# Inverse square roots of the norms by a power on GpSimd and one Newton step

## Chip, cores and metric

The kernel runs on one core of one Trainium2 chip. The metric is the device time of one execution in microseconds (us), a median of repeated runs. Engines are named as in the profile: PE is TensorE (PEld its weight loads), DVE is VectorE, ACT is ScalarE, POOL is GpSimd, SP is the engine that issues most transfers.

## The reference, cut to what matters

The input x has 8 batches of 1024 rows of 256 values, in float32. An attention block is followed by a feed-forward block, each with a residual and a layer norm after it.

```python
q, k, v = x @ Wq.T + bq, x @ Wk.T + bk, x @ Wv.T + bv      # 16 heads of 16
q = softmax(q, axis=-1)                                    # over the 16 values of a head
k = softmax(k, axis=-2)                                    # over the 1024 rows
out = q @ (k.T @ v)                                        # per head
out = (out - mean(out)) * rsqrt(var(out) + EPS) * ln_g + ln_b
x = layernorm(x + out @ Wo.T + bo)

h = layernorm(x) * ln1_g + ln1_b
h = gelu(h @ ternary(w1).T + b1)                           # 256 -> 1024, exact gelu
h = layernorm(h) * ln2_g + ln2_b
x = layernorm(x + h @ ternary(w2).T + b2)                  # 1024 -> 256
```

`ternary(w)` rounds w over its mean absolute value to -1, 0 or 1 and scales it back. Every layer norm needs 1/sqrt(var + EPS) of each row.

## The kernel before

**Tiling.** A batch lies in SBUF with 128 rows on the partitions and NT = 8 row tiles of 256 columns. Four tiles are a block of 512 rows, so there are 16 blocks, two per batch. All matmuls are in float32 or its fp32r form.

**Order.** The order of all instructions is written out by hand (`manual_schedule`). One loop runs over 18 iterations i. In the first 16, block i gets its keys, queries and the product of keys and x; in even iterations the state of the batch before is finished; and block i - 2 gets its attention output (`attend`). Iterations 16 and 17 have only `attend` left, and the feed-forward's slots are mixed in.

**The norm's steps.** `attend` puts a short generator (`bn_stats`, then `bn_aggr`) in the queue `soon`. When both blocks of a batch are through, a generator `norm(b, tiles)` is put in the queue `later`. It issues one VectorE instruction per step: var + EPS for all tiles (L519), `rsqrt` for these n = 8 columns (tiles `ny_o`, `nt_o`), then for each tile the scaled residual add (L526), statistics (L532) and their aggregate (L534), then two rows of variances (L539, L541), `rsqrt` for these 2n = 16 columns (`ny_y`, `nt_y`; the second half serves the feed-forward's entry norm), then sh (L546) and two products for rs2 (L549, L551). After it, ScalarE applies the norm to the tiles (L772), a few at a time through `apply(n)`. Norms of batches 0 to 6 have 8 tiles, that of batch 7 comes in two halves of 4. `more(n)` advances the queues by n steps, `soon` first; the step that ends a generator also advances the next queue. An even iteration of the attention hands out 1, 4, 4, 4, 1, 4, 6, 6, 6, 1 and 6 steps.

**Around it.** In an attention iteration VectorE takes the maxima of the keys (mx, L326), from which mb and nb (L333, L335) give the bias of ScalarE's exponentials (ekT, L338), whose transposes (pte, L351) TensorE waits for. It adds the bias of the queries (q, L368) out of PSUM, takes their maxima (qm, L377) and sums (rq, L388 and L390). GpSimd subtracts the maxima (L378), multiplies by the inverse sums (L391) and issues a transfer that adds a constant row to x (L855). A preparation of the quantised weights is spread over the first ten iterations (`prep`; among it mean of L179 and the columns of L194).

**Feed-forward.** Blocks go through slots s, eight per block, numbered by m = s + 11 for the hidden layer. A slot holds matmuls into the hidden layer (ph, L615 and L619), ScalarE's gelu (L620), a turn of a hidden tile (pt, L643) split into a high and a low part (ScalarE L568, VectorE L569), and the product with the second weights (pf, L657). At m % 8 = 0 `enter` gives GpSimd two passes over the next block (L576, L579). At m % 8 = 5 and 6 the input of the next block is turned (pth, L592) and split in the same way (hT, L568 and L569). At s % 8 = 2 `norms` issues `rsqrt` without a break for one vector of 8 columns: four of the result's norm of the block before, four of the hidden norm (`ny_f`, `nt_f`). At s % 8 = 3 `finish` applies the former on GpSimd (four times L670) and stores the block; sc and ms (L706, L708) come from the latter. After the last slot one more `rsqrt` of 4 columns (`ny_last`) leads to the last `finish`.

There are 35 inverse square roots in all: 9 of `ny_o`, 9 of `ny_y`, 16 of `ny_f` and `ny_last`.

Of the kernel before, what the change touches and what calls it, by code (L numbers as in the profile page):

```python
# [7 lines left out]

F32 = mybir.dt.float32
I32 = mybir.dt.int32  # L10
F32R = mybir.dt.float32r
AF = mybir.ActivationFunctionType
ALU = mybir.AluOpType
AX = mybir.AxisListType

P = 128
EPS = 1e-5
ROUND = 12582912.0
RSQRT_SEED = float(0x5F3759DF)


@with_exitstack
def attn_ffn_postln_kernel(
# [11 lines left out]
    nc = tc.nc  # L35
# [6 lines left out]
    NT = N // P  # L42
# [4 lines left out]
    const = ctx.enter_context(tc.tile_pool(name="const", bufs=1))  # L47
# [59 lines left out]
    def finish_all(steps):  # L107

        while True:
            try:  # L110
                next(steps)
            except StopIteration as end:
                return end.value

    def rsqrt(v, name):


        n = v.shape[1]
        y = small.tile([P, 2 * NT], F32, tag="ny", name=f"ny_{name}")[:, :n]
        t = small.tile([P, 2 * NT], F32, tag="nt", name=f"nt_{name}")[:, :n]  # L120
        yi = y.bitcast(I32)
        nc.vector.tensor_scalar(yi, v.bitcast(I32), 1, None, ALU.logical_shift_right)
        yield
        nc.vector.tensor_scalar(yi, yi, -1.0, RSQRT_SEED, ALU.mult, ALU.add)
        for step in range(3):
            yield
            nc.vector.tensor_tensor(t, y, y, ALU.mult)  # L127
            yield
            nc.vector.scalar_tensor_tensor(t, t, -0.5, v, ALU.mult, ALU.mult)
            yield  # L130
            nc.vector.scalar_tensor_tensor(y, t, 1.5, y, ALU.add, ALU.mult)
        return y


# [379 lines left out]
    def norm(b, tiles):  # L514
# [4 lines left out]
        nc.vector.tensor_scalar(v, mvo[b][:, lo:hi, 1], EPS, None, ALU.add)  # L519
        yield  # L520
        rs = yield from rsqrt(v, f"o_{b}_{lo}")
        yield
        mv = small.tile([P, NT, 2], F32, tag="mvy", name=f"mvy_{b}_{lo}")[:, :n, :]
# [17 lines left out]
        nc.vector.tensor_scalar(v[:, n:], mv[:, :, 1], 1.0 + EPS, EPS * EPS, ALU.mult, ALU.add)  # L541
        yield
        rs = yield from rsqrt(v, f"y_{b}_{lo}")
        yield
        sh = small.tile([P, NT], F32, tag="shy", name=f"shy_{b}_{lo}")[:, :n]
# [143 lines left out]
    def norms(s):  # L689

        i, j = s // HC, s % HC
        if j in (0, 1) and i > 0:
            result_stats(i - 1, 2 * j)
            result_stats(i - 1, 2 * j + 1)
        if i == len(blocks):
            return
        if j == 2:
            v = small.tile([P, 2 * G], F32, tag="nv", name=f"nv_f_{i}")
            nc.vector.tensor_scalar(v[:, :G], mv[i][:, :G, 1], EPS, None, ALU.add)
            nc.vector.tensor_scalar(v[:, G:], mv[i][:, G:, 1], 1.0 / HID, EPS, ALU.mult, ALU.add)  # L700
            rs[i] = finish_all(rsqrt(v, f"f_{i}"))
        if j == 3:
            if i > 0:
                finish(i - 1, mv[i][:, :G, 0], rs[i][:, :G])
            sc[i] = small.tile([P, G], F32, tag="sc", name=f"sc_{i}")
            nc.vector.tensor_scalar(sc[i], rs[i][:, G:], inv2, None, ALU.mult)  # L706
            ms[i] = small.tile([P, G], F32, tag="ms", name=f"ms_{i}")
            nc.vector.tensor_tensor(ms[i], sc[i], mv[i][:, G:, 0], ALU.mult)  # L708
        if j in (4, 5):
            add_mean(i, 2 * j - 8)  # L710
            add_mean(i, 2 * j - 7)
# [204 lines left out]
```

## Time and profile before

| what | value |
|---|---|
| time, median of 3 runs | 741.25 us (739.79 to 741.45) |
| profiled execution: its own time | 739.53 us |
| profiled execution: span of the instructions | 737.8 us |
| mean granted TensorE clock | 0.978 |
| TensorE matmul / weight load busy | 690.7 / 549.1 us |
| VectorE busy | 583.7 us, 1642 instructions |
| ScalarE busy | 441.0 us |
| GpSimd busy | 194.8 us, 156 instructions |
| HBM traffic | 31 GB/s over the span |

How to read the profile: a line of a group names the source line, the engine, the operation, output and inputs, the count, the busy time and the mean of one in ns, then the idle time of that engine just before and what released it. A line of the order of time gives the start in us, the time in us, and the instruction, with the idle time before it and its releaser in brackets. A line of the chain of waits gives the start, the time, and which instruction held the end back then. The attention runs to about 348 us, the last `attend` and the first feed-forward slots to about 420, the feed-forward alone to about 712.

### The profile page before, as it was taken

The numbers are of one execution on the slowest core, as the hardware profiler recorded it, in microseconds if no ns is written. First come the engines' busy times: TensorE is split into PE (matmuls) and PEld (weight loads), VectorE is DVE, ScalarE is ACT, GpSimd is POOL, SyncE is SP. The second block draws the span as 40 slices with busy tenths as digits, with TensorE's granted clock in tenths as the row PEclk, the third lists the DMA queues.
The fourth block names the chain that finished last, engine by engine and source line by source line (L and its number), as shares of the span: only waits on it lengthen the run. The fifth ranks groups of instructions, "written<-read, shape, count | busy, mean of one in ns | idle before, by whom it ended". The sixth has DMA issues, their size and how long they took to land.

```text
span 737.8 us, 10770 instructions
## 1 busy us (share of the span) xinstructions
PE 690.7 (94%) x3780; PEld 549.1 (74%) x3780; DVE 583.7 (79%) x1642; ACT 441.0 (60%) x970; POOL 194.8 (26%) x156
## 2 busy tenths in 40 slices
PE   6899999979989999997998899999999999999992
PEld 4677766757657777765767788888888888888882
DVE  1667798877988959797898778877878877887686
ACT  2344436535364545546787667777777677677760
POOL 1232223121221222244420033332133333123112
PEclk9999999989999999998999899999999999999997
DMA  8833103222120111210100000000000000000001
GB/s 328 306 72 58 29 15 72 51 36 51 21 33 13 29 29 28 30 24 11 24 0 2 1 29 30 30 29 30 1 29 30 28 29 30 2 28 29 30 30 58
DMA packets 17238, 32.03 MB, mean 43 GB/s; under 512 B 1344, under 2 KB 12608, under 8 KB 16288
## 3 DMA queue, kind: packets, MB, share of 16 engines
q0 software_dynamic: 8608, 8.79, 7.9%
q1 hardware_dynamic: 7344, 21.50, 7.7%
q10 hardware_dynamic: 1232, 1.06, 0.4%
q8 instruction: 30, 0.49, 0.3%
q14 instruction: 24, 0.20, 0.1%
HBM read 14.56 MB, written 8.39 MB: 31 GB/s over the span
## 4 chain that ended last, share of the span: by engine, by line
PE 70%; DVE 23%; ACT 3%; DMA 2%; issue 2%; POOL 0%; POOLq 0%; ACTq 0%; DVEq 0%
PE pf L657 16%; PE ph L615 14%; PE pt L643 7%; PE po L498 6%; PE pq L364 5%; PE pa L407 5%; PE pk L322 5%; PE ph L619 3%; DVE x L526 3%; DVE st_y L532 2%; DMA wqkv_sb<-in_wqkv_dram 2%; PE pth L592 2%; PE ptq L301 1%; PE ptx L301 1%; DVE sto L508 1%
## 5 line engine op out<-in xcount | busy, mean ns | idle before, releaser
L657 PE MATMUL pf<-t,u 128*128 128x256 f32 x1024 | 157.5, 295 | 4.0 <-DVE x L716 3.6
L615 PE MATMUL ph<-t,hT 128*128 128x512 f32 x512 | 144.2, 403 | 1.2 <-DVE hT L569 1.2
L657 PEld LDWEIGHTS pf<-t,u 128*128 128x128 f32 x1024 | 131.9, 191 | 9.8 <-issue 5.8
L569 DVE SCALAR_TENSOR_TENSOR u<-pt,cols_sb,u 128x512 fp32r<-128x512 f32 x128 | 95.5, 746 | 45.6 <-ACT u L568 44.2
L620 ACT ACTIVATE h<-ph 128x512 f32<-128x512 f32 x128 | 76.5, 598 | 83.9 <-PE ph L619 73.7
L670 POOL TENSOR_SCALAR x<-x,ny_f,sh 128x256 f32<-128x256 f32 x60 | 38.1, 650 | 261.0 <-DVE sh L667 261.0
L615 PEld LDWEIGHTS ph<-t,hT 128*128 128x128 f32 x512 | 88.6, 189 | 15.3 <-DVE hT L569 1.9
L498 PE MATMUL po<-sm,qT 128*128 128x384 f32 x256 | 97.3, 505 | 0.1
L568 ACT ACTIVATE u<-pt,cols_sb 128x512 fp32r<-128x512 f32 x128 | 87.5, 684 | 8.3 <-PE pt L643 7.6
L643 PE MATMUL pt<-ident,h 128*128 128x128 f32 x512 | 78.1, 275 | 4.2 <-DVE u L569 2.5
L632 ACT ACTIVATE sq<-h,mvh 128x1024 f32<-128x1024 f32 x64 | 73.8, 1153 | 5.5 <-DVE mvh L624 5.5
L643 PEld LDWEIGHTS pt<-ident,h 128*128 128x128 f32 x512 | 61.6, 141 | 19.9 <-DVE hT L569 6.0
L378 POOL TENSOR_TENSOR q<-q,qm 128x1024 f32<-128x1024 f32 x16 | 30.8, 1926 | 150.1 <-DVE qm L377 90.6
L364 PE MATMUL pq<-wqkv_sb,xT 128*128 128x256 f32 x256 | 60.6, 380 | 0.8 <-DMA wqkv_sb<-in_wqkv_dram 0.8
L322 PE MATMUL pk<-xT,wqkv_sb 128*128 128x512 f32 x128 | 61.3, 603 | 0.0
L407 PE MATMUL pa<-x,ek 128*128 128x256 f32 x256 | 61.1, 382 | 0.0
L498 PEld LDWEIGHTS po<-sm,qT 128*128 128x128 f32 x256 | 46.5, 198 | 19.4 <-issue 2.1
L391 POOL TENSOR_TENSOR q<-q,rq 128x1024 f32<-128x1024 f32 x16 | 30.9, 1933 | 108.2 <-DVE rq L390 59.0
L407 PEld LDWEIGHTS pa<-x,ek 128*128 128x128 f32 x256 | 48.9, 192 | 13.1 <-issue 0.6
L364 PEld LDWEIGHTS pq<-wqkv_sb,xT 128*128 128x128 f32 x256 | 47.9, 190 | 12.7 <-issue 3.1
L680 DVE SCALAR_TENSOR_TENSOR x<-g2sum,ms,x 128x256 f32<-128x256 f32 x64 | 56.9, 927 | 0.0
L338 ACT ACTIVATE ekT<-pk,nb 128x512 f32<-128x512 f32 x32 | 21.7, 682 | 56.5 <-DVE nt_y L127 35.6
(144 smaller groups left out, 1151.9 us busy)
## 6 DMA issues: line engine op xcount, KB each, us to landing
x<-crow POOLq DMA_DIRECT2D x16, 512.0 KB, 5.5
out_dram<-x SPq DMA_DIRECT2D x16, 512.0 KB, 2.6
x<-in_x_dram SPq DMA_DIRECT2D x7, 1024.0 KB, 10.2
x<-in_x_dram SPq DMA_DIRECT2D x2, 512.0 KB, 5.6
wm_w<-in_w_dram SPq DMA_DIRECT2D x4, 256.0 KB, 8.0
wq_w<-in_w_dram SPq DMA_DIRECT2D x4, 256.0 KB, 2.5
wm_w<-in_w_dram SPq DMA_DIRECT2D x8, 128.0 KB, 2.1
wq_w<-in_w_dram SPq DMA_DIRECT2D x8, 128.0 KB, 2.0
```

The costliest lines, as they stand in the source:

```text
L322: nc.tensor.matmul(pk, wqkv_sb[:, k, C + c * P : C + (c + 1) * P], xT[i][:, k, :], start=(k == 0), stop=(k == KC - 1),)
L364: nc.tensor.matmul(pq[:, n, :], xT[i][:, k, (t + n) * P : (t + n + 1) * P], wqkv_sb[:, k, 0:C], start=(k == 0), stop=(k == KC - 1),)
L407: nc.tensor.matmul(pa[i][:, c, :], ek[i][:, t, c * P : (c + 1) * P], x_of(i)[:, t, :], start=(t == 0), stop=(t == G - 1),)
L498: nc.tensor.matmul(po[:, c * P : c * P + P + C], qT[i][:, c, t * P : (t + 1) * P], sm[b][:, c, :], start=(c == 0), stop=(c == KC - 1), ski ...
L568: nc.scalar.activation(hi, src, AF.Copy, scale=gain)
L569: nc.vector.scalar_tensor_tensor(lo, src, gain, hi.bitcast(F32), ALU.mult, ALU.subtract)
L615: nc.tensor.matmul(ph, hT[i][s][:, k, t * P : (t + 1) * P], t1[:, k, cols_j], start=(s == 0 and k == 0), stop=False,)
L620: nc.scalar.activation(h[i][t][:, cols_j], ph, AF.Gelu, accum_out=h[i, t][:, half : half + 1])
L632: nc.scalar.activation(sq, h[i][t], AF.Square, bias=mv[i][:, G + t, 0:1], accum_out=mv[i][:, G + t, 1:2])
L643: nc.tensor.transpose(pt[:, t * P : (t + 1) * P], h[i][t][:, j * P : (j + 1) * P], ident)
L657: nc.tensor.matmul(pf[i][t // 2][:, t % 2, :], u[s][:, n, t * P : (t + 1) * P], t2[:, j, :], start=(j == 0 and t % 2 == 0 and n == 0), sto ...
L680: nc.vector.scalar_tensor_tensor(x_t, g2sum, ms[i][:, t : t + 1], x_t, ALU.mult, ALU.add)
```

## The change

`rsqrt(v)` gave a vector 1/sqrt(v) by an integer shift and a subtraction on the bits and three Newton steps of three instructions, eleven VectorE instructions with ten breaks between them. It now gives v to the power -1/2 in one GpSimd instruction, with a constant tile of -0.5 as the exponent, and one Newton step of three VectorE instructions, with three breaks. All 35 inverse square roots go through it.

```diff
-RSQRT_SEED = float(0x5F3759DF)
...
+    mhalf = const.tile([P, 2 * NT], F32, name="mhalf")
+    nc.vector.memset(mhalf, -0.5)
+
     def rsqrt(v, name):
         n = v.shape[1]
         y = small.tile([P, 2 * NT], F32, tag="ny", name=f"ny_{name}")[:, :n]
         t = small.tile([P, 2 * NT], F32, tag="nt", name=f"nt_{name}")[:, :n]
-        yi = y.bitcast(I32)
-        nc.vector.tensor_scalar(yi, v.bitcast(I32), 1, None, ALU.logical_shift_right)
-        yield
-        nc.vector.tensor_scalar(yi, yi, -1.0, RSQRT_SEED, ALU.mult, ALU.add)
-        for step in range(3):
-            yield
-            nc.vector.tensor_tensor(t, y, y, ALU.mult)
-            yield
-            nc.vector.scalar_tensor_tensor(t, t, -0.5, v, ALU.mult, ALU.mult)
-            yield
-            nc.vector.scalar_tensor_tensor(y, t, 1.5, y, ALU.add, ALU.mult)
+        nc.gpsimd.tensor_tensor(y, v, mhalf[:, :n], ALU.pow)
+        yield
+        nc.vector.tensor_tensor(t, y, y, ALU.mult)
+        yield
+        nc.vector.scalar_tensor_tensor(t, t, -0.5, v, ALU.mult, ALU.mult)
+        yield
+        nc.vector.scalar_tensor_tensor(y, t, 1.5, y, ALU.add, ALU.mult)
         return y
```

More of the change, by code (lines that the diff above doesn't have):

```diff
@@ L9 @@
 F32 = mybir.dt.float32
-I32 = mybir.dt.int32
 F32R = mybir.dt.float32r
```

## The prediction

> **What bounds the kernel now.** I read the page's busy shares first, then its chain of waits, then what waited for whom, and last the order of time on VectorE and TensorE around each inverse square root.
>
> ```profile
> PE 690.7 (94%) x3780; PEld 549.1 (74%) x3780; DVE 583.7 (79%) x1642; ACT 441.0 (60%) x970; POOL 194.8 (26%) x156
> ...
> PE 70%; DVE 23%; ACT 3%; DMA 2%; issue 2%; POOL 0%; POOLq 0%; ACTq 0%; DVEq 0%
> ```
>
> TensorE ends most of the span, but VectorE holds 23% of the chain. GpSimd is on it only at the very end. So the value of shorter VectorE work depends on the stage. The small instructions themselves, by shape:
>
> ```profile
> L127 DVE TENSOR_TENSOR nt_f<-ny_f 128x8 f32<-128x8 f32 x48 | 8.0, 167 | 1.6
> L131 DVE SCALAR_TENSOR_TENSOR ny_y<-nt_y,ny_y 128x16 f32<-128x16 f32 x21 | 3.7, 175 | 0.5
> L378 POOL TENSOR_TENSOR q<-q,qm 128x1024 f32<-128x1024 f32 x16 | 30.8, 1926 | 150.1 <-DVE qm L377 90.6 <-DVE z L425 59.5
> L905 POOL MEMSET const-float32-1.0<- 128x1 f32 x1 | 0.1, 98 | 0.0
> ```
>
> No power is in this trace. These rows give an instruction of the old chain (0.17 us), an ordinary two-input GpSimd pass (1.93 us for 1024 columns) and GpSimd's smallest instruction (0.10 us). In the feed-forward stage (420 to 712 us) one group of eight slots takes 21.9 us; this is the place of its chain, VectorE first, then the weight loads:
>
> ```profile
> 595.54 0.17 DVE L122 TENSOR_SCALAR ny_f<-nv_f 128x8 int32<-128x8 int32 x1
> 595.75 0.17 DVE L124 TENSOR_SCALAR ny_f<-ny_f 128x8 int32<-128x8 int32 x1
> ...
> 597.56 0.17 DVE L131 SCALAR_TENSOR_TENSOR ny_f<-nt_f,ny_f 128x8 f32<-128x8 f32 x1
> 597.65 0.74 DVE L569 SCALAR_TENSOR_TENSOR hT<-pth,gs,hT 128x512 fp32r<-128x512 f32 x1
> ...
> 598.45 0.42 PEld L643 LDWEIGHTS pt<-ident,h 128*128 128x128 f32 x4 [0.28 <-DVE hT L569]
> ```
>
> Eleven dependent instructions start 0.20 us apart. The hT pass queued behind them frees the PSUM buffer for which TensorE's next transposes wait. The transposes then take 0.51 us of the chain instead of 0.44: TensorE loses 0.07 us per group and has no slack. A longer chain costs its whole excess here; a shorter one gains at most 0.07.
>
> **What the skill says.** "GPSIMD Engine Reference", section "Elementwise — side-by-side cycle accounting": about 2.6 cycles per element for two inputs; the trace's 1926 ns / 1024 = 1.88 ns is 2.3 cycles at the page's 1.2 GHz, so it agrees roughly. It has no price for a power. "SBUF — State Buffer", "Who interferes with whom": a GpSimd instruction and a VectorE instruction with two SBUF inputs exclude each other. The trace agrees: the pass L526 takes 1.83 us beside the GpSimd pass at 96.08 us and 0.45 us elsewhere. "TensorE: Matmul & The Clock Gate", "HAM oscillation": idle gaps above some 3.4 us halve TensorE's clock. Here gaps of 3.70 us (before 162.2) and 3.50 us (before 334.4) are followed by half-speed stretches of 6.8 us (mean clock 0.85 and 0.87 in these windows); but so are pairs of shorter gaps (2.26 and 0.34 at 204, 3.4 us; 1.31 and 2.52 before 410, 6.8 us), so the trace is less lenient.
>
> **The round trip.** VectorE's qm ends at 95.92 and GpSimd starts at 96.08: 0.16 us. GpSimd's pass ends at 211.58 and ScalarE starts at 211.62: 0.04. So an inverse square root removes 8 x 0.20 = 1.60 us of VectorE time and adds a stall L = 0.20 + d, d being the power. Three Newton instructions stay. The constant's one memset at the start counts as nothing: VectorE is busy for 0.31 of the first 10 us, which are loads (uncovered, 0.2 us at most, the like of `ones`).
>
> Bounds of d: floor, a memset's 0.10 plus the row's 1.9 ns per column, 0.12 us. For the middle, the same skill page, "Performance pitfalls for Q7 kernels", prices a dependent fp32 step at 4 cycles. My assumption is some 20 such steps per column (a logarithm, a product, an exponential), 16 partitions of a core side by side: estimate 20 x 4 / 1.2 GHz = 67 ns per column, so d = 0.10 + 0.067n: 0.37, 0.63, 1.17 us for 4, 8, 16 columns and L = 0.57, 0.83, 1.37. Ceiling: the 16 partitions one after the other, 16 x 0.067 x 8 = 8.6 us. I take the middle since the passes of this trace do run partitions side by side. The same page's "Instruction dispatch" adds some 6 us once if code must first be loaded; I leave it to the range.
>
> **Part by part.**
>
> *Attention, batches 0 to 5.* A norm is a list of steps handed out by `more(n)`. Before: 1+11+24+2+11+3 = 52; after: 38. An even iteration hands out 43, of which four serve `attend`'s statistics: 39. So before, the second root spills into the odd iteration; after, the whole norm fits the even one. That iteration loses nine old instructions (1.80) and gains two stalls (8 and 16 columns: 2.20), three Newton instructions (0.60) and sh and two rs2 (0.50): +1.50. Idle time ahead of q L368 takes 0.40 plus 0, 0.71, 0.1, 0.65, 1.04 for norms 0 to 4. The second root's last instruction now meets GpSimd's multiply L391 under the lock, for about 0.45 more. Net +1.55, +0.8, +1.4, +0.9, +0.5. Next in line are mx, nb, the exponentials and TensorE's pte transposes. Their slack is nothing in norms 0, 1, 2 (TensorE already waits 0.55, 0.24, 2.26 us), but 1.7 in norm 3 (exponential done 248.34, pte at 250.08) and 0.5 in norm 4: +3.8 us in all. The odd iteration loses 13 instructions (2.6 us); I give it back 1.5, mostly from the 3.70 us gap, which ends with VectorE's mean L179.
>
> Norm 5 is different:
>
> ```profile
> 327.77 3.10 DVE ny_y L122
> 330.87 1.20 DVE mx L326 x2
> 332.09 1.17 DVE mb L333
> ```
>
> L122 sits 3.1 us under the lock of the feed-forward's first pass on GpSimd (`enter`, 328.39 to 330.83); TensorE then idles 3.50 us. After, the norm is over before that pass, mx can run beside it, and nb comes some 2.3 us sooner. I add half of the 3.4 us that the slow clock costs. Stage: 3.8 - 1.5 - 2.3 - 1.7 = **-1.7**.
>
> *The change of stage, 348 to 420.* Norm 6, two half norms and the first feed-forward root: L minus 1.60 is -0.77, -0.23, -1.03, -0.77, -1.03, -0.77, -0.77, together -5.4 us of VectorE time. The powers also stand between `enter`'s passes in GpSimd's queue, which now cannot run ahead and lock VectorE (L127 took 2.21 us at 355.70): some -2. TensorE's gaps here that end with VectorE are 1.2 (at 372), 1.7 (395), 1.3 and 2.5 (407 to 410), and the slow clock costs 3.4: 10 us. ScalarE also waits 2.64 and 3.61 us for shy L546, which comes earlier. I take **-5.5**. What a power can be late behind: an `enter` of 4.4 us, once or twice here.
>
> *Feed-forward.* GpSimd is idle for 14.9 us before each finish, so the power starts at once: 13 x 0.07 = **-0.9**. What ends the wait next is TensorE itself.
>
> *Tail.* Two chains lie bare on the path:
>
> ```profile
> 729.60 0.17 DVE L122 TENSOR_SCALAR ny_last<-nv_last 128x4 int32<-128x4 int32 x1
> ...
> 731.58 0.16 DVE L131 SCALAR_TENSOR_TENSOR ny_last<-nt_last,ny_last 128x4 f32<-128x4 f32 x1
> 731.77 0.16 DVE L667 SCALAR_TENSOR_TENSOR sh<-mvh,ny_last 128x4 f32<-128x4 f32 x1
> 732.11 2.16 POOL L670 TENSOR_SCALAR x<-x,ny_last,sh 128x256 f32<-128x256 f32 x4 [7.12 <-DVE sh L667]
> ```
>
> -0.77 (at 719.4) and -1.03: **-1.8**.
>
> Sum: -9.9 us on the profiled execution's 739.53 (span 737.8 and 1.7 around it). The median, 741.25, is 1.7 above it; less 9.9 gives 731.4, rounded to **732 us**.
>
> **Rivals.** *A slow power (ends slower).* Each 0.1 us on d for 8 columns (0.2 for 16) costs about 0.9 in attention, 0.6 at the change of stage and 0.2 in the tail: 1.7 us, so the gain is gone at d = 1.2 us. Above d = 1.4 every feed-forward group pays too: at d = 2 some 24 us more than the forecast plus 15 x 0.6 = 9, or 765 us. One partition after the other (8.6 us) costs 16 x 7.2 = 115 in the feed-forward alone and about 160 in the norms: over 1000 us. For it: VectorE truly waits, and no row excludes it. Against it: all GpSimd rows here are near line rate. *A floor-priced power*: L about 0.3 everywhere: some 6 us better than forecast, 726, as the gaps of the first 420 us can only be closed once. *Hidden anyway*: if TensorE's gaps in the first 420 us are re-formed by other waits (ScalarE's, the lock's), FFN and tail alone give -2.7 and the +3.8 eats it: 741 to 742, no change.
>
> **How the numbers follow.** Forecast with its floor case 0.66; within 0.2% (1.5 us, about what a measurement can tell from no change) 0.04; a power of 1.3 to 3 us 0.18; above that 0.12. The range reaches from below the floor case, 721, to a power near 1.9 us, 760; about 0.2 is left out, mostly above.
>
> **What would show it.** Right: a power of 128x8 near 0.6 us; VectorE idle about 0.8 before each y*y; 280 VectorE instructions fewer (35 roots of 8, one memset more) and 35 powers on GpSimd; no pte gap near 334; the transposes at 598 no longer waiting for hT; the tail's chain 1.2 us. Wrong: powers above 1.2 us, pt waiting for hT for longer, TensorE's clock at half in more stretches, or a power queued behind `enter`.

## The result and the profile after

The changed kernel takes **761.00 us** (median of 6 runs, 760.43 to 764.10), the kernel before 739.53 us (median of 6 runs; the 741.25 above was the median of the first three). The ratio is 1.0291, 95% interval 1.0272 to 1.0311: 21.5 us slower, where a gain, to 732 us, was forecast. The profiled execution took 761.63 us with a span of 759.9 us.

The page of the changed kernel: busy time by engine, then the chain of waits by engine.

```profile
PE 697.7 (92%) x3780; PEld 552.0 (73%) x3780; DVE 551.2 (73%) x1363; ACT 442.7 (58%) x970; POOL 259.4 (34%) x191
...
PE 63%; DVE 24%; POOL 5%; ACT 3%; DMA 2%; issue 2%; ACTq 0%; POOLq 0%; DVEq 0%
```

VectorE lost 32.5 us of busy time and the 279 instructions that it was to lose; GpSimd got its 35. Yet GpSimd, which had 0% of the chain of waits, now has 5%, and the share of TensorE fell from 70% to 63%. Three of the groups on GpSimd, by shape, name the reason (mean of one in ns after the busy time; line numbers are 3 lower than before):

```profile
L122 POOL TENSOR_TENSOR ny_f<-nv_f,mhalf 128x8 f32<-128x8 f32 x16 | 26.3, 1646 | 178.9 <-DVE nv_f L697 178.9
L122 POOL TENSOR_TENSOR ny_y<-nvy,mhalf 128x16 f32<-128x16 f32 x7 | 20.3, 2904 | 53.6 <-DVE nvy L538 53.6
L122 POOL TENSOR_TENSOR ny_last<-nv_last,mhalf 128x4 f32<-128x4 f32 x1 | 1.0, 1007 | 4.7 <-DVE nv_last L744 4.7
```

A power takes 1.01, 1.65 and 2.90 us for 4, 8 and 16 columns, where the prediction took 0.37, 0.63 and 1.17. All 35 together take 64.6 us. What waited for whom (total in us, times, longest) shows that VectorE does wait for nearly all of it, and TensorE behind it:

```profile
DVE nt_f L124 <- POOL ny_f L122: 28.3, 16, 1.8
DVE nt_y L124 <- POOL ny_y L122: 22.9, 9, 3.0
PE pte L348 <- ACT ekT L335: 22.0, 10, 7.6
DVE nt_o L124 <- POOL ny_o L122: 10.9, 9, 1.8
```

TensorE's wait for the exponentials (pte) was 7.4 us in all before:

```profile
PE pte L351 <- ACT ekT L338: 7.4, 7, 3.5
```

TensorE's clock suffered too, which the prediction had named as a sign of being wrong: the trace shows it at half speed for 47.6 us in all, 33.8 before (mean granted clock 0.970, 0.978 before), and the same 3780 matmuls are busy for 697.7 us, 690.7 before. How much of the loss passes through the clock was not separated from the waits.

**Where the time went.** The same instructions were found in the order of time of both traces: GpSimd's transfer of the constant row, once in each attention iteration, and VectorE's sh of each feed-forward finish. The differences of their starts give a table by stage, for the profiled executions:

| stretch | prediction | changed kernel |
|---|---|---|
| first four iterations (no norm yet) | 0 | +1.3 |
| norms 0 to 5, to 348 us of before | -1.7 | +15.0 |
| change of stage, to the first finish at 424 us of before | -5.5 | +6.0 |
| feed-forward, eleven groups of eight slots | -0.9 for 13 | +0.3 |
| the rest | -1.8 | -0.5 |
| span | -9.9 | +22.1 |

The +1.3 stands before the first norm. It comes and goes in the other runs (-0.3 to +2.7; -0.2 in one with the same powers and the same constant), so it is not the change's. The clock goes with it: in the changed kernel and in seven of the twelve experiments TensorE is at half speed for 3.4 or 6.8 us from about 20 to 22 us on, and these are 0.9 to 2.7 us late there; the other five and the kernel before have no such stretch, and these five lie within 0.3 us of it.

### The profile page after: what moved, and what is told of

It is laid out like the page before. It is cut to its first block, busy times and chain, and to the rows that moved or that the text cites. A ratio compares the mean times of both kernels' runs of the same rounds, so it can differ in the third digit from the quotient of the medians.

```text
span 759.9 us, 10498 instructions
## 1 busy us (share of the span) xinstructions
PE 697.7 (92%) x3780; PEld 552.0 (73%) x3780; DVE 551.2 (73%) x1363; ACT 442.7 (58%) x970; POOL 259.4 (34%) x191
## 4 chain that ended last, share of the span: by engine, by line
PE 63%; DVE 24%; POOL 5%; ACT 3%; DMA 2%; issue 2%; ACTq 0%; POOLq 0%; DVEq 0%
PE pf L654 15%; PE ph L612 13%; PE pt L640 7%; PE po L495 6%; PE pa L404 5%; PE pk L319 4%; DVE x L523 4%; PE ph L616 3%; DVE st_y L529 3%; POOL ny_y L122 3%; DMA wo_sb<-in_wo_dram 2%; PE pq L361 2%; POOL ny_o L122 2%; PE pte L348 1%; DVE ny_y L128 1%
## 5 line engine op out<-in xcount | busy, mean ns | idle before, releaser
L495 PE MATMUL po<-sm,qT 128*128 128x384 f32 x256 | 99.6, 515 | 0.0
L122 POOL TENSOR_TENSOR ny_f<-nv_f,mhalf 128x8 f32<-128x8 f32 x16 | 26.3, 1646 | 178.9 <-DVE nv_f L697 178.9
L769 ACT ACTIVATE x<-x,shy,ny_y 128x256 f32<-128x256 f32 x64 | 36.1, 597 | 47.3 <-DVE shy L543 47.3
L500 ACT COPY o<-po 128x256 f32<-128x256 f32 x64 | 23.8, 372 | 49.7 <-PE po L495 49.6
```

Source lines behind the costliest of these rows:

```text
L122: nc.gpsimd.tensor_tensor(y, v, mhalf[:, :n], ALU.pow)
L495: nc.tensor.matmul(po[:, c * P : c * P + P + C], qT[i][:, c, t * P : (t + 1) * P], sm[b][:, c, :], start=(c == 0), stop=(c == KC - 1), ski ...
```

## The experiments

Three theories were held against each other. **Stall**: the power is long, and each wait for it is time on the path. **Order** (called the packing theory later): the new root has three breaks in place of ten, so a norm has 38 steps in place of 52 and lies in one iteration, where VectorE has no room, whatever the root is computed with. **Lock**: GpSimd, while it raises to a power, slows VectorE's own instructions.

| kernel | time, us | ratio to before, 95% interval |
|---|---|---|
| power in the attention norms only | 759.02 | 1.0263 (1.0246 to 1.0279) |
| power in the feed-forward and the last norm only | 742.15 | 1.0029 (1.0015 to 1.0044) |
| old chain, 38 steps | 756.26 | 1.0229 (1.0210 to 1.0248) |
| seed and one Newton step, 38 steps | 734.15 | 0.9932 (0.9905 to 0.9960) |
| seed and one Newton step, 52 steps | 729.54 | 0.9865 (0.9836 to 0.9895) |
| power, 52 steps | 746.42 | 1.0080 (1.0054 to 1.0107) |
| power hidden, 46 steps | 736.61 | 0.9955 (0.9937 to 0.9973) |
| power hidden, 52 steps | 732.74 | 0.9906 (0.9880 to 0.9932) |
| product in place of the power, 38 steps | 731.31 | 0.9896 (0.9873 to 0.9918) |
| power issued twice, 38 steps | 830.10 | 1.1217 (1.1175 to 1.1259) |
| two Newton steps, 46 steps | 741.49 | 1.0029 (1.0016 to 1.0042) |
| two Newton steps, 52 steps | 734.20 | 0.9932 (0.9908 to 0.9955) |

### Which half of the change

The new root in the norms of the attention (names `o` and `y`), the old one elsewhere; and the reverse (`"fl"` in place of `"oy"`).

```diff
+        if name[0] in "oy":
+            nc.gpsimd.tensor_tensor(y, v, mhalf[:, :n], ALU.pow)
...
+            return y
```

> Power and one Newton step only for the 18 roots of the attention's norms, the old chain for the 17 of the feed-forward and the end. Theory of the stall: all of the loss is in the norms, since the feed-forward's chain is only 0.12 us longer: 759 to 762 us. Rival, the feed-forward pays too (0.25 us in each of 15 groups): 756 to 758 us.

> Power and one Newton step only for the 16 roots of the feed-forward and the last one, the old chain in the attention's norms. Theory of the stall: as before, 738 to 741 us: the feed-forward's chain is 0.12 us longer, the last one 0.4 shorter. Rival, the feed-forward pays its excess of 0.25 us in each of 15 groups: 742 to 744 us.

Measured: 759.02 and 742.15 us, +19.1 and +2.2 on the 739.92 of before. The loss is in the norms. The second lies in the range of the rival, in which each feed-forward group pays; but in its trace 1.7 us are there before the first norm, as in the table above, and the eleven groups together grow by only 0.5. So the feed-forward's 16 powers, 26.3 us of GpSimd, cost next to nothing.

### The order alone, and a short chain in the same order

The old eleven instructions, but in one step up to the last Newton step, so with the three breaks of the changed kernel and no power on GpSimd; and the same with the seed and a single Newton step (two left out). The diff is against the changed kernel. The first kernel has the three added Newton lines twice; in the second they are missing.

```diff
-        nc.gpsimd.tensor_tensor(y, v, mhalf[:, :n], ALU.pow)
+        yi = y.bitcast(I32)
+        nc.vector.tensor_scalar(yi, v.bitcast(I32), 1, None, ALU.logical_shift_right)
+        nc.vector.tensor_scalar(yi, yi, -1.0, RSQRT_SEED, ALU.mult, ALU.add)
+        nc.vector.tensor_tensor(t, y, y, ALU.mult)
+        nc.vector.scalar_tensor_tensor(t, t, -0.5, v, ALU.mult, ALU.mult)
+        nc.vector.scalar_tensor_tensor(y, t, 1.5, y, ALU.add, ALU.mult)
...
         yield
         nc.vector.tensor_tensor(t, y, y, ALU.mult)
```

> The eleven old instructions, exact as before, but with the three breaks of the changed kernel: seed and two Newton steps in the first step, the last one broken as in the changed kernel. Nothing on GpSimd. Theory of the stall: VectorE gets 2.5 us more in the even iteration and 2.6 less in the odd one; where TensorE has no slack (norms 0, 1, 2) that costs about 2 us each, given back in part: 740 to 748 us. Rival, the order: it alone makes the slowdown, 755 to 763 us.

> The power is replaced by the two instructions of the old seed on VectorE, in one step; one Newton step stays, so the roots are less exact. Every break and so the order of all other work is that of the changed kernel. Theory of the stall (VectorE stands still for 1.8 us at 8 columns and 3.1 at 16, and the attention's even iterations have no room for it): two stalls of 4.9 us in a norm become 0.8, so about 728 us (722 to 736), 3.6 us gaps before pte gone. Rival, the order (38 steps put the whole norm into the even iteration): the order is unchanged, so 752 to 761 us.

Measured: 756.26 us with the old chain, 734.15 with the short one. The first is the surprise, as the theory of the stall expected 740 to 748 and that of the order 755 to 763: the work of the kernel before, instruction for instruction, loses 16.3 us by standing in fewer steps. The second shows that it is not the packing as such: with 1.0 us of VectorE in place of 2.2 per root, the packed norm gains 5.8 us. What counts is how much time the packed norm holds, and a wait fills it as instructions do.

### The length of the power

From below: GpSimd multiplies the same two tiles, so the trip, the wait and the steps stay, but not the length (the root is then not computed).

```diff
-        nc.gpsimd.tensor_tensor(y, v, mhalf[:, :n], ALU.pow)
+        nc.gpsimd.tensor_tensor(y, v, mhalf[:, :n], ALU.mult)
```

> GpSimd multiplies the same two tiles instead of raising to the power, so the norms' roots are not computed; everything else of the changed kernel stays, the trip to GpSimd and back, the wait and the 38 packed steps. It asks whether the prediction's sum holds where the power is as short as its floor (some 0.1 us, wait 0.3). If the length of the power is what failed, this gives 724 to 732 us, near the prediction's floor case of 726. If the trip to GpSimd or the packing costs by itself, whatever the length, 740 us or more.

From above: the power is issued twice.

```diff
         nc.gpsimd.tensor_tensor(y, v, mhalf[:, :n], ALU.pow)
+        nc.gpsimd.tensor_tensor(y, v, mhalf[:, :n], ALU.pow)
```

> Each power is issued twice on GpSimd, so that every wait of VectorE for it grows by 1.65 us (8 columns), 2.9 us (16 columns) or 1.0 us (the last, 4 columns). If each wait is on the path that sets the end, the time grows by 9 x 1.65 + 9 x 2.9 + 16 x 1.65 + 1.0 = 68 us, to about 829 us. If the FFN has slack of at least one power in each group, as the equal times of its groups before and after the change suggest, the attention's 41 us come alone, 795 to 805 us. If the attention's waits are mostly beside other limits too, under 785.

Measured: 731.31 and 830.10 us. The groups on GpSimd with the product, then the waits with two powers:

```profile
L122 POOL TENSOR_TENSOR ny_f<-nv_f,mhalf 128x8 f32<-128x8 f32 x16 | 3.2, 202 | 192.6 <-DVE nv_f L697 192.6
L122 POOL TENSOR_TENSOR ny_y<-nvy,mhalf 128x16 f32<-128x16 f32 x7 | 1.5, 221 | 55.3 <-DVE nvy L538 55.3
```

```profile
DVE nt_f L125 <- POOL ny_f L123: 55.8, 16, 3.5
DVE nt_y L125 <- POOL ny_y L123: 47.1, 9, 6.0
PEld pt L641 <- DVE hT L567: 33.4, 14, 5.5
```

The products take 7.2 us together, the powers 64.6, the doubled powers 128.9. So the first 57.4 us of length cost 29.7 us (761.00 - 731.31), a half, and the next 64.3 cost 69.1, all of it and some more (mean granted clock 0.949, 0.970 with one power). The expectation's 68 us for the second power was near. Its idea that the feed-forward might hide one more power failed: a group of eight slots took 21.71 us with the product, 21.87 before, 21.90 with one power and 23.64 with two (mean of eleven), the last 1.74 more for 1.65 of length. In the third line TensorE waits for hT 14 times; in the changed kernel that was 9.4 us in all. The feed-forward's chain was thus just filled by one power of 8 columns.

### The same waits, the old steps

Seven empty breaks behind the last instruction of the attention's roots give the norm its 52 steps again.

```diff
         nc.vector.scalar_tensor_tensor(y, t, 1.5, y, ALU.add, ALU.mult)
+        for _ in range(7):
+            yield
         return y
```

> The changed kernel with 7 empty breaks at the end of each attention root, so that a norm has its 52 steps again and lies over the same two iterations as before the change; VectorE still stands and waits for each power. If the loss comes from long waits meeting packed steps, this gives 741 to 747 us: each wait stays (1.8 and 3.0 us), but the steps around it lie in their old places. If the waits alone cost, wherever they stand, it stays at 757 to 761. If only the number of breaks counted it would be 732 to 738.

> The seed from the bits and one Newton step on VectorE (two Newton steps left out, so the root is less exact), with 7 empty breaks at the end of each attention root: 52 steps in a norm as before the change. The chain is as short as in the run with the seed and one Newton step in 38 steps, which took 734. If packing itself costs, this is faster than that by 3 or more, 726 to 731 us. If a short chain has nothing to lose from packing, 732 to 737.

Measured: 746.42 us for the power, 729.54 for the short chain. Empty breaks alone take 14.6 us of the changed kernel's 21.5 us loss away. The mechanism is in the order of time on VectorE at norm 5 of the first of these:

```profile
326.41 0.16 DVE L540 TENSOR_SCALAR nvy<-mvy 128x8 f32<-128x8 f32 x1
326.48 1.27 DVE L325 TENSOR_REDUCE mx<-pk 128x1 f32<-128x512 f32 x2
327.79 0.16 DVE L332 TENSOR_TENSOR mb<-mx,bkv 128x2 f32<-128x2 f32 x1
329.58 0.17 DVE L124 TENSOR_TENSOR nt_y<-ny_y 128x16 f32<-128x16 f32 x1 [1.63 <-POOL ny_y L122]
```

With 52 steps the second power is the last step of its iteration. VectorE takes the next iteration's key maxima (mx, mb) while GpSimd computes and waits 1.63 us. With 38 steps it waited 3.02 us at this place:

```profile
339.60 0.17 DVE L124 TENSOR_TENSOR nt_y<-ny_y 128x16 f32<-128x16 f32 x1 [3.02 <-POOL ny_y L122]
```

Over all nine second roots the wait fell from 22.9 to 13.1 us. By the stages of the table above, norms 0 to 5 now take -1.0 us against before, not +15.0; the change of stage keeps +5.8 of its +6.0; what holds it there was not separated.

### The power hidden

Empty breaks right behind the power (3 in the roots of `o`, 5 in those of `y`) let VectorE do other steps while GpSimd computes; in the feed-forward the Newton step comes one slot after the power. The second kernel has, besides, the rest of the seven breaks at the end.

```diff
-        yield
+        for _ in range(1 + wait):
+            yield
...
-            rs[i] = finish_all(rsqrt(v, f"f_{i}"))
+            rs[i] = rsqrt(v, f"f_{i}")
+            next(rs[i])
         if j == 3:
+            rs[i] = finish_all(rs[i])
```

> The power and its one Newton step stay, but VectorE gets other work while GpSimd computes: 3 empty breaks behind the power in the roots of 8 columns of the attention's norms, 5 in those of 16, and in the FFN the power is issued one step of the loop earlier than the Newton step. The waiting theory (VectorE stands still for 1.65 or 2.9 us in a crowded stretch, that is what costs) expects the waits for the powers nearly gone and 728 to 738 us. The theory that the packing of the whole norm into one iteration costs, whatever it holds, expects 742 to 752, since 46 of the 52 old breaks are back only in part. The rival that the power disturbs VectorE by the shared lock while it runs expects over 745 and longer VectorE instructions beside it.

> The power hidden behind 3 or 5 empty breaks and one step of the FFN loop, which took 737 us with 46 steps in a norm, now with the remaining empty breaks at the end of each root, 52 steps. If packing has a price of its own, 729 to 735 us. If the hidden power is all there is to gain, 735 to 738.

Measured: 736.61 and 732.74 us. The waits that are left in the second, and its chain of waits by engine:

```profile
DVE nt_y L125 <- POOL ny_y L122: 4.6, 4, 2.5
DVE nt_o L125 <- POOL ny_o L122: 2.9, 2, 1.8
```

```profile
PE 73%; DVE 16%; ACT 4%; DMA 3%; POOL 2%; issue 1%; ACTq 0%; POOLq 0%; DVEq 0%
```

The three kinds of wait that came to 62.1 us are down to 8.3 (0.8 us of it for `nt_f`), and the same 35 powers now stand in a kernel that is 0.94% **faster** than before. The lock theory falls with it. VectorE's instructions with two inputs from SBUF, those that the lock would hold, take beside a power what they take elsewhere. In the second kernel, GpSimd's power and VectorE's pass of the preparation that lies wholly beside it:

```profile
111.40 3.01 POOL L122 TENSOR_TENSOR ny_y<-nvy,mhalf 128x16 f32<-128x16 f32 x1 [0.18 <-DVE nvy L541]
112.21 0.75 DVE L225 SCALAR_TENSOR_TENSOR brow<-hi,sel,b 128x512 fp32r<-128x512 f32 x1
```

The other pass of brow, with no power beside it, takes 0.75 us too. The six mb that lie beside a power take 0.16 us each, where one took 1.17 beside the pass of `enter` (in the prediction). The 15 passes of hT beside a power, with one input from PSUM, take 0.75 us each, as elsewhere. In the first kernel the largest excess of one that lies wholly beside a power is 0.07 us, on one mb. Between the two kernels lie only empty breaks, and 3.9 us.

### Two Newton steps on VectorE

The kernel before with two Newton steps in place of three, without and with three empty breaks at the end of the root (the last two lines of the diff are in the second kernel alone).

```diff
-        for step in range(3):
+        for step in range(2):
...
+        for _ in range(3):
+            yield
```

> The kernel before with two Newton steps in place of three (the root is less exact), 46 steps in a norm: no GpSimd, chains of eight instructions. Between the old chain in few breaks (756, slower) and the seed with one Newton step in few breaks (734): the tail and the FFN gain some 2 us, the rest depends on where the steps fall. If shorter chains gain more than packing loses, 731 to 739; if packing decides, 742 to 750.

> The same two Newton steps with 3 empty breaks at the end of each attention root, 52 steps as before the change. The seed with one Newton step in the old spacing took 729.5; each Newton step is 0.6 us of VectorE per root, so half of the 10 us gained comes back: 733 to 737 us. If steps in their old places hide the third Newton step, 729 to 732.

Measured: 741.49 and 734.20 us. The first lies between the two ranges that were expected, so neither was met: three instructions fewer in each of 35 roots end 0.29% **above** the kernel before (the lower edge of the interval is 0.16%), since 46 steps place the norm badly; the same instructions in 52 steps gain 5.5 us. The 7.3 us between them are the order's.

**Fastest.** The seed with one Newton step in the old steps, 729.54 us (ratio 0.9865), less exact in the root; with a root as exact as the change's, the hidden power in the old steps, 732.74 us (0.9906).

## Why the prediction was wrong

**The power's length, the step that failed first.** The sum rested on 0.63 and 1.17 us for 8 and 16 columns, from an assumed 20 dependent steps per column at the 4 cycles that the Trainium skill prices ("GPSIMD Engine Reference", "Performance pitfalls for Q7 kernels"). The three shapes fit 0.37 us plus 0.158 us per column, 2.4 times the assumed slope. The page's price of a step is neither confirmed nor refuted, as no run shows how many steps a power takes; the count was my guess. The prediction's own threshold, 1.2 us, lay below the 1.65 that came, so this is its first rival, a slow power; it had given lengths of 1.3 to 3 us a chance of 0.18.

**How much of it the wrong length explains.** With the assumed durations the powers would take 25.1 us together. From the product's 7.2 us (731.31) over the real 64.6 (761.00) to the doubled 128.9 (830.10) the time rises ever more steeply, so an estimate for 25.1 us from these runs lies between 731.3 and the straight line's 740.6. By this estimate the length explains at least 20 of the 29 us of error; no run had that very length. The product also tests the prediction's rival of a power priced at its floor: the waits are at most 0.38 us, where it said about 0.3, but the gain is 8.4 us, where its 726 meant some 15. So the sum has faults besides the length.

**Attention, norms 0 to 4: right formula, wrong inputs.** With the real lengths in its stalls (0.20 + 1.65 and 0.20 + 2.90, together 4.95 in place of 2.20) the step's sum for the even iterations gives +4.3, +3.6, +4.2, +2.0, +2.8, together 16.7. The trace shows +3.6, +4.4, +3.1, +2.0, +2.3, together 15.4. With two powers the sum gives 39.5 and the trace 39.4. With the product it would give a gain of 1.8, and the trace shows none: the sum prices added waits, not gains. The odd iterations gave back 4.0 us, not 1.5.

**Norm 5: wrong in itself.** A gain of 4.0 us was forecast, as the norm would be over before `enter`. It cost 3.6, and the gap before pte that was to vanish grew. The order of time after, VectorE and then GpSimd:

```profile
341.91 1.69 DVE L128 SCALAR_TENSOR_TENSOR ny_y<-nt_y,ny_y 128x16 f32<-128x16 f32 x1
343.63 3.20 DVE L543 SCALAR_TENSOR_TENSOR shy<-mvy,ny_y 128x8 f32<-128x8 f32 x1
346.75 0.15 DVE L546 TENSOR_TENSOR rs_all<-ny_y 128x8 f32<-128x8 f32 x1
346.94 2.30 DVE L548 TENSOR_TENSOR rs_all<-rs_all,nvy 128x8 f32<-128x8 f32 x1
349.17 1.27 DVE L323 TENSOR_REDUCE mx<-pk 128x1 f32<-128x512 f32 x2
```

```profile
341.63 1.93 POOL L388 TENSOR_TENSOR q<-q,rq 128x1024 f32<-128x1024 f32 x1 [2.07 <-DVE rq L387]
343.51 1.36 POOL L852 DMA_DIRECT2D x<-crow  x1
344.34 2.45 POOL L573 TENSOR_TENSOR h<-x,rs_all 128x1024 f32<-128x1024 f32 x1
346.88 2.35 POOL L576 TENSOR_TENSOR x<-x,bout 128x1024 f32<-128x1024 f32 x1
```

The norm's last instructions stand behind rq in VectorE's order, and rq also releases GpSimd's multiply (L388), behind which the two passes of `enter` (L573, L576) follow at once. So L128, L543 and L548 run beside these and take 1.69, 3.20 and 2.30 us in place of some 0.17; mx stands behind them all, and TensorE (first before the change, then after):

```profile
334.38 0.47 PE L351 MATMUL pte<-ident,ekT 128*128 128x128 f32 x1 [3.50 <-ACT ekT L338]
351.76 0.48 PE L348 MATMUL pte<-ident,ekT 128*128 128x128 f32 x1 [7.58 <-ACT ekT L335]
```

This does not need a long power. With the short product L128, L543 and L548 take 1.69, 3.16 and 2.30 us in the same place, the norm costs 0.5 us, and the gap is 4.33 us:

```profile
332.45 0.48 PE L348 MATMUL pte<-ident,ekT 128*128 128x128 f32 x1 [4.33 <-ACT ekT L335]
```

So at least 4.5 of the 7.6 us between forecast and measurement at this norm are not the length's; with the length the gap grows from 4.33 to 7.58 us. The prediction had counted steps and durations, but not asked which instruction releases the passes that the moved steps meet. The Trainium skill's rule on the lock ("SBUF — State Buffer", "Who interferes with whom") was quoted there and agrees with these durations; apart from the one instruction that meets the multiply, it was applied to the place that the instructions left and not to the one they came to.

**Change of stage.** -5.5 forecast, +6.0 measured, and -1.9 with the product. The assumed lengths lie between the product's and the real ones, so at most 8 of the 11.5 us of error come with the length, and at least 3.6 are optimism in the gaps added up to 10 us. Which of these gaps stayed for which reason was not separated. No power stood late behind an `enter`: the longest wait for one was 3.0 us, for 2.9 of length.

**Feed-forward.** The group after, to be held against the one shown before the change:

```profile
618.03 1.65 POOL L122 TENSOR_TENSOR ny_f<-nv_f,mhalf 128x8 f32<-128x8 f32 x1 [11.13 <-DVE nv_f L697]
619.72 0.17 DVE L124 TENSOR_TENSOR nt_f<-ny_f 128x8 f32<-128x8 f32 x1 [1.76 <-POOL ny_f L122]
...
620.21 0.74 DVE L566 SCALAR_TENSOR_TENSOR hT<-pth,gs,hT 128x512 fp32r<-128x512 f32 x1
...
621.00 0.42 PEld L640 LDWEIGHTS pt<-ident,h 128*128 128x128 f32 x4 [0.43 <-DVE hT L566]
```

The weight loads wait 0.43 us, 0.28 before: the chain is 0.15 longer, not shorter. The step's rule, that a longer chain costs its whole excess, held for the second power (1.74 us per group for 1.65), but 0.15 cost only 0.03, so there is a slack of about 0.1 us that it denied. A shorter chain gains more than the 0.07 said: 0.16 with the product.

**Tail.** -1.8 forecast, -0.5 measured. The step's form was right and its size follows the length: the last stall is 0.20 + 1.01 = 1.21 us (1.13 of it idle, below) where 0.57 was taken, and that of the other bare chain, of 8 columns, 1.85 where 0.83 was taken; that is 1.7 of difference, against 1.3 found.

```profile
753.28 0.16 DVE L124 TENSOR_TENSOR nt_last<-ny_last 128x4 f32<-128x4 f32 x1 [1.13 <-POOL ny_last L122]
```

**The slope.** The prediction priced 0.1 us on 8 columns and 0.2 on 16 at 1.5 us for attention and change of stage, some 0.6 of the length. Up to the first finish, the step from product to power cost 25.5 us for 35 of length (0.73), the step to two powers 43.6 for 38.7 (1.13). With its own slope, even the true length would have given 752 us: 10.2 tenths of a us x 1.7 = 17.3, and 15 x 0.25 = 3.75, on -9.9.

## What to carry to other kernels

An operation that no trace prices is worth a kernel of its own before anything is built on it: here a trace of a single power would have turned the sign. When work moves to another engine in an order written by hand, what counted here is what stands between its issue and its first reader; the same 35 powers lost 2.9% with nothing between, and the kernel gained 0.9% with steps of other work there and the norm's old number of steps. And the number of breaks in a generator is a setting like any other: empty breaks alone moved this kernel by 3.9 to 14.6 us, so a change that shortens a chain is to be measured with the old number of steps too.

## What the runs showed of the hardware

In this case a power on GpSimd takes 0.37 us plus 0.158 us per column of float32 over 128 partitions (a line through 1.01, 1.65 and 2.90 us at 4, 8 and 16 columns). It is alike in the first call and in later ones: the prediction had left 6 us for a first load of code in its range, but the first power of the changed kernel took 1.67 us and VectorE waited 1.16 us for it. A product of the same small tiles takes 0.19 to 0.22 us, almost whatever the columns.

A power hardly slowed VectorE's instructions beside it: 0.75 us for hT, which reads PSUM, in 15 of 15, and 0.75 us for brow, 128x512 with two inputs from SBUF, in the three kernels in which it lies wholly beside a power (both kernels with the hidden power, and the power with 52 steps); the largest excess found is 0.07 us. The exclusion that the prediction quotes for a GpSimd instruction and a VectorE instruction with two SBUF inputs thus did not show for a power, while it did for GpSimd's large two-input passes (up to 3.20 us for L543). These three powers of 16 columns were themselves somewhat longer, 3.01 to 3.09 us in place of 2.90.
